# Two of four TensorE transposes moved to a later place in each iteration of a state-space mixer

## The chip, the cores and the metric

The kernel runs on one core of a Trainium2 chip. The metric is the device time of one execution in microseconds, taken as the median of several runs. Three runs of the kernel before gave 1757.22, 1758.23 and 1759.07 us.

## What is computed

The reference is one block of a recurrent model: a layer norm, a mixer of the Mamba-2 kind (`_L0_attn_ref`), a gated feed-forward branch with ternary weights, and their product added to the input. Cut to what bears on the change:

```python
xn = _layernorm(x, axis=-1)                       # x: 4 batches x 256 positions x 512
zxbcdt = xn @ in_proj_w.T                         # gate, xBC, dt
conv = conv1d(xBC, conv_w, 4 taps, causal)
x, B, C = split(silu(conv + conv_b))              # x: 128 heads of 64
xs = x * dt[..., None]
Gm = einsum(C, B)                                 # scores of a chunk
Y_diag = einsum(Gm * L, xs)                       # L: decay from position to position
Y_off = ...                                       # what earlier chunks hand on
y = (Y_diag + Y_off + D * x) * silu(gate)
y = y * rsqrt(mean(y * y over a group) + EPS) * norm_w
s = y @ out_proj_w.T
g = silu(ffn(xn))
return x + s * g
```

All of it is float32. The products `L @ xs` need `xs` with positions on the partitions, while the convolution leaves `x` with channels on the partitions. So `x` is transposed on TensorE, and this is what the change is about.

## The kernel before

**Stages.** The kernel first does the layer norm, the feed-forward branch, the steps dt and the scores of all groups (`front`, to about 310 us). Then comes the main loop (line 766): 64 iterations, one for each tile of 128 of the 8192 inner channels, i = 0 to 63. A tail with no loop over tiles finishes the output projection. The order of all work is written out by hand (`tc.manual_schedule()`): each engine carries out its instructions in the order in which the lines issue them, and waits on semaphores where data or a buffer is not ready.

**One iteration** overlaps three tiles. For tile i it projects gate and x, for tile i-1 (`old`) it computes the recurrence, for tile i-2 (`older`) it gates and squares. From i = 10 on it also does a piece of the output projection of an earlier group (`og >= 0`): the seven block products of one batch in a pair of iterations, four in the even one and three in the odd one. In even iterations VectorE first makes four sums for it (`left_sums`, lines 701 to 704). In every eighth iteration (i = 10, 18, ... 58) TensorE also sums squares in 16 small matmuls (`norm_sums`, L683).

**The projection** of a tile is a fast product of 2 x 2 blocks (Winograd's form of Strassen's method) with seven block products in place of eight. A block product is two calls and appears in the profile as four matmul instructions of 128x512 (`product`, L173). They go into three PSUM banks px, pq and pz. The seven, by their usual numbers, and in the order of issue on TensorE, are:

- P1 = a11 x11 into px; ScalarE copies px to pz (L820)
- P5 = s1 t1 into pq
- P6 = s2 t2, added into px; ScalarE copies px out to gT (L830)
- first half of P2 = a12 x21, added into pz (k = 0, line 836)
- **four transposes of "block 0"** of tile i-1: the first 128 positions of each of the four batches, into the bank tp (`transposed`, L624)
- P7 = s3 t3, added into px: it may write only when L830 has read px (line 845)
- second half of P2 (k = 1, line 846); ScalarE copies px out to xpad (L847)
- P4 = a22 t4, added into px: it may write only when L847 has read px (line 877)
- P3 = s4 x22, added into pq: it may write only when VectorE has read pq (L870, `xpad <- xpad + pq`)
- four transposes of "block 1" of tile i-1 (`values_1`), into the same PSUM bank as block 0

**Who uses the transposes of block 0.** `values_0` (L632) on VectorE scales tp twice; it is issued behind L870. The bank (pool `ps_t`) has one buffer, so block 1's transposes wait for L632.

**Iterations 1 to 9** (`lead`, i - 1 < LEAD) differ: the last activation of tile i-1 and both exponentials of the decay stand on ScalarE between the copies L820 and L830 or right behind, with loads of ScalarE's function tables.

**VectorE** in an iteration, in order: gating (L672), a decay scan (L612), `meet` (L618, L619, twice each), in even iterations the four sums, L870, L632 twice, L886, the scaling of block 1 (L641), the convolution taps (L181), the sums for the next tile's factors, and another scan.

Before the change, the place in the loop reads:

```python
                product(pz, a12, x21, False, (0,))
            if old:
                tp0 = transposed(xTs[i - 1], 0)
```

Of the kernel before, what the change touches and what calls it, by code (L numbers as in the profile page):

```python
# [43 lines left out]
F32 = mybir.dt.float32  # L44
# [6 lines left out]
P = 128  # L51
NB = 4
# [29 lines left out]
def mixer_ffn(ctx: ExitStack, tc: tile.TileContext, x, in_w, conv_w, conv_b, dt_bias, a_log, d_col,  # L82
# [7 lines left out]
    ps_t = ctx.enter_context(tc.tile_pool(name="ps_t", bufs=1, space=PSUM))  # L90
# [76 lines left out]
    def by_batch(v):  # L167
        return v.rearrange("p (b l) -> p b l", l=L)

    def product(pp, a, b, start, ks=range(KT // 2)):  # L170

        for k in ks:
            nc.tensor.matmul(pp, a[:, k, :], b[:, k, :], start=start and k == 0,  # L173
                             stop=k == KT // 2 - 1, skip_group_check=not start)
# [442 lines left out]
    def meet(m, off):  # L617
        nc.vector.tensor_mul(m, m, gm[:, 0:T])  # L618
        nc.vector.tensor_mul(off, off, gm[:, T:])  # L619

    def transposed(xT, c):
        tp = ps_t.tile([P, NB, P], F32, name="tp", tag="t")
        for b in range(NB):
            nc.tensor.transpose(tp[:, b, :], xT[:, b, c * P:(c + 1) * P], ident)  # L624
        return tp

# [11 lines left out]
    def values_1(ct, xT):  # L638
        tp = transposed(xT, 1)
        v = xsp.tile([P, NB, 2, HD], F32, name="v")  # L640
        nc.vector.tensor_tensor(  # L641
            v, tp.rearrange("p b (h d) -> p b h d", d=HD),
            dt[:, 1, :, 2 * ct:2 * ct + 2].unsqueeze(3).to_broadcast([P, NB, 2, HD]), ALU.mult)
        return v

    def y_begin(ct, xT):

        ps = []
        for i in range(2):
            py = ps_y.tile([P, 2, L], F32, name="py", tag="y")  # L650
            nc.scalar.mul(py, xT[:, 2 * i:2 * i + 2, :], dcol[:, ct:ct + 1])
            ps.append(py)
        return ps
# [107 lines left out]
    with tc.manual_schedule():  # L761
        nc.sync.dma_start(gm, scores[0])
        ms, offs = {0: load_rows(0)}, {0: load_off(0)}
        xTs, gTs, yps, wos, rights, toms = {}, {}, {}, {}, {}, {}
        sqacc = rs = ya = outs = left = nxt = ob = sa = sb = sc = None
        for i in range(CT):
            r, g = i % PER_G, i // PER_G
            here, old, older = True, i >= 1, i >= 2
# [66 lines left out]

                product(pz, a12, x21, False, (0,))
            if old:
                tp0 = transposed(xTs[i - 1], 0)
                meet(ms[i - 1][0], offs[i - 1][0])
                meet(ms[i - 1][1], offs[i - 1][1])  # L840
                if r == 0 and here:
                    nc.sync.dma_start(gm, scores[g])
                yps[i - 1] = y_begin(i - 1, xTs[i - 1])
            if here:
                product(px, s3, t3, False)
                product(pz, a12, x21, False, (1,))
                nc.scalar.copy(xpad_h[1], by_batch(px))  # L847
            if og >= 0 and on == 0:
                sd = norm_sums(sqacc)
# [101 lines left out]
        decay_exp(ms[last][1])  # L951
        py = y_begin(last, xTs[last])
        vs = values_0(last, transposed(xTs[last], 0))
        for m, off in zip(ms[last], offs[last]):
            meet(m, off)
# [123 lines left out]
```

## Time and profile before

| | |
|---|---|
| median of three runs | 1758.23 us (1757.22 to 1759.07) |
| the profiled execution | 1757.47 us, span 1755.8 us |
| TensorE clock granted over the span | 0.999 |
| TensorE waiting to load weights of px until ScalarE's copy L847 | 36.8 us in 57 waits |
| four transposes, from the first's start to the next product's | 0.44 us |
| an odd iteration, 909.58 to 930.70 us | 21.1 us |
| an even iteration, 930.70 to 953.56 us | 22.9 us |

The page of the profile gives busy time by engine, the chain of work that ended last, and groups of instructions. PE is TensorE's matmuls, PEld its weight loads (which run ahead of the matmuls), DVE is VectorE, ACT ScalarE. A timeline line has the start in microseconds from the start of the span, the length, engine, line of the kernel, operation, output and inputs, shapes and count; in brackets stands how long the engine was idle before and what released it. [...] An idle of 0.24 us before a weight load of a 128x512 matmul is the normal interval of the stream.

### The profile page before, as it was taken

Reading aid. Unit: us, or ns where it says so; the run is one execution under the profiler, and the core shown is the slowest. Engines: PE = TensorE matmul, PEld = TensorE weight load, DVE = VectorE, ACT = ScalarE, POOL = GpSimd, SP = SyncE. Lnnn points to the kernel's source line nnn. Section 1 sums busy time; section 2 is a strip of 40 time slices with the busy share of each in tenths; the row PEclk is TensorE's granted clock in tenths of the full one; section 3 lists DMA queues with packets and bytes.
Section 4 is the critical chain, followed back from the end, with each engine's and each line's share of the span. In section 5 each row is a group of like instructions: output and inputs, shape, how many; then the busy total and the mean of one; then the engine's idle time right before and its main releaser. Section 6 shows DMA issues by size and latency. Waiting matters only on the chain.

```text
span 1755.8 us, 22590 instructions
## 1 busy us (share of the span) xinstructions
PE 1725.9 (98%) x8494; PEld 1105.4 (63%) x8494; DVE 1449.8 (83%) x1742; ACT 1065.8 (61%) x1418; POOL 197.3 (11%) x238
## 2 busy tenths in 40 slices
PE   9999999999999999999999999999999999999999
PEld 6566667444456666666666666666666666666677
DVE  5757665699988898889888988888888988888876
ACT  4544333577766666666666666666666666666640
POOL 3221121000000000111011101110111011101110
PEclk9999999999999999999999999999999999999999
DMA  6254553567756666776677667766777677767785
GB/s 228 79 189 154 208 180 113 191 209 233 217 197 207 201 206 190 209 201 185 204 210 201 193 183 213 200 199 183 211 201 214 165 213 201 213 165 212 213 233 170
DMA packets 164091, 342.16 MB, mean 195 GB/s; under 512 B 15376, under 2 KB 55952, under 8 KB 163984
## 3 DMA queue, kind: packets, MB, share of 16 engines
q1 hardware_dynamic: 141296, 287.78, 47.4%
q0 software_dynamic: 22688, 52.96, 17.0%
q8 instruction: 67, 1.10, 0.3%
q14 instruction: 40, 0.33, 0.1%
HBM read 236.08 MB, written 76.28 MB: 178 GB/s over the span
## 4 chain that ended last, share of the span: by engine, by line
PE 86%; DVE 10%; ACT 2%; issue 2%; DMA 0%; SPq 0%; ACTq 0%; DVEq 0%
PE px L173 25%; PE po L721 22%; PE pq L173 13%; PE py L665 9%; PE pz L173 6%; PE pp L285 4%; PE tp L624 3%; DVE m L612 2%; PE pf L293 2%; DVE xT L181 2%; PE pg L460 1%; DVE cT L181 1%; PE pv L683 1%; DVE m L618 1%; DVE bT L181 1%
## 5 line engine op out<-in xcount | busy, mean ns | idle before, releaser
L612 DVE TENSOR_TENSOR_SCAN m<-m,after 128x1024 f32<-128x1024 f32 x128 | 292.1, 2282 | 0.0
L173 PE MATMUL px<-xc,w 128*128 128x512 f32 x576 | 279.3, 607 | 4.6 <-ACT xpad L424 2.4
L181 DVE SCALAR_TENSOR_TENSOR xT<-xpad,cw,xT 128x1024 f32<-128x1024 f32 x192 | 246.2, 1282 | 4.6
L721 PE MATMUL po<-wo,ya 128*128 128x256 f32 x768 | 176.5, 379 | 0.0
L173 PEld LDWEIGHTS px<-xc,w 128*128 128x128 f32 x576 | 99.2, 190 | 115.1 <-issue 69.4
L665 PE MATMUL py<-m,v 128*64 128x128 f32 x2048 | 160.6, 276 | 3.7 <-DVE v L641 3.7
L618 DVE TENSOR_TENSOR m<-m,gm 128x1024 f32<-128x1024 f32 x128 | 154.8, 1209 | 1.4 <-ACT m L615 1.4
L721 PEld LDWEIGHTS po<-wo,ya 128*128 128x128 f32 x768 | 141.5, 190 | 17.1 <-issue 0.2
L905 POOL DMA_DIRECT2D sqacc<-sq x54 | 46.1, 853 | 897.5 <-ACT sq L861 894.0
L173 PE MATMUL pz<-xnT,w 128*128 128x512 f32 x288 | 145.8, 592 | 0.0
L173 PE MATMUL px<-xnT,w 128*128 128x512 f32 x288 | 142.0, 615 | 0.4 <-DMA w<-in_in_w 0.4
L173 PE MATMUL px<-xc,s 128*128 128x512 f32 x288 | 135.8, 594 | 4.5 <-ACT cpad L424 2.0
L173 PE MATMUL pq<-xnT,s 128*128 128x512 f32 x288 | 136.2, 595 | 3.4 <-DVE xpad L870 3.4
L615 ACT ACTIVATE m<-m 128x1024 f32<-128x1024 f32 x128 | 135.4, 1058 | 0.7
L173 PE MATMUL pq<-xc,s 128*128 128x512 f32 x288 | 135.4, 592 | 0.2 <-DMA s<-early 0.2
L665 PEld LDWEIGHTS py<-m,v 128*64 128x64 f32 x2048 | 116.9, 137 | 25.6 <-issue 19.7
L721 PE MATMUL po<-tw,sy 128*128 128x256 f32 x512 | 115.9, 379 | 0.0
L624 PEld LDWEIGHTS tp<-ident,xT 128*128 128x128 f32 x512 | 63.8, 141 | 67.4 <-issue 53.2
L721 PEld LDWEIGHTS po<-tw,sy 128*128 128x128 f32 x512 | 97.2, 190 | 13.2
L870 DVE TENSOR_TENSOR xpad<-xpad,pq 128x512 f32<-128x512 f32 x64 | 43.7, 683 | 68.5 <-ACT xpad L847 68.5
L830 ACT COPY gT<-px 128x512 f32<-128x512 f32 x64 | 37.3, 583 | 103.5 <-PE px L173 103.5
L173 PEld LDWEIGHTS px<-xc,s 128*128 128x128 f32 x288 | 54.2, 190 | 72.1 <-issue 65.5
(181 smaller groups left out, 3105.2 us busy)
## 6 DMA issues: line engine op xcount, KB each, us to landing
m<-rows SPq DMA_DIRECT2D x128, 512.0 KB, 6.5
w<-in_in_w SPq DMA_DIRECT2D x133, 256.0 KB, 6.9
mo<-rows SPq DMA_DIRECT2D x128, 256.0 KB, 7.2
gated<-yg SPq DMA_DIRECT2D x64, 512.0 KB, 8.3
ya<-gated SPq DMA_DIRECT2D x30, 1024.0 KB, 7.1
sqacc<-sq POOLq DMA_DIRECT2D x54, 512.0 KB, 5.6
wo<-in_out_w SPq DMA_DIRECT2D x64, 256.0 KB, 7.2
acc<-sa POOLq DMA_DIRECT2D x23, 512.0 KB, 5.9
```

Source lines behind the costliest of these rows:

```text
L173: nc.tensor.matmul(pp, a[:, k, :], b[:, k, :], start=start and k == 0, stop=k == KT // 2 - 1, skip_group_check=not start)
L181: nc.vector.scalar_tensor_tensor(xT, xpad[:, :, k:k + L], cw[:, i, k:k + 1], xT, ALU.mult, ALU.add)
L285: nc.tensor.matmul(pp, w[:, k * P:(k + 1) * P], part[:, k, :], start=(k == 0 and part is xh), stop=(k == KT - 1 and part is xl))
L612: nc.vector.tensor_tensor_scan(m, m, after, 0.0, ALU.add, ALU.mult)
L615: nc.scalar.activation(m, m, AF.Exp)
L618: nc.vector.tensor_mul(m, m, gm[:, 0:T])
L624: nc.tensor.transpose(tp[:, b, :], xT[:, b, c * P:(c + 1) * P], ident)
L665: nc.tensor.matmul(py[d, q * P:(q + 1) * P], v[:, b, h, :], m, start=False, stop=stop, skip_group_check=True)
L721: nc.tensor.matmul(po, a[:, k, :], b[:, k, :], start=start and k == 0, stop=k == HG - 1, skip_group_check=not start)
L830: nc.scalar.copy(gT[:, HALF:], px)
L870: nc.vector.tensor_add(xpad_h[1], xpad_h[1], by_batch(pq))
L905: nc.gpsimd.dma_start(sqacc, sq, accum_op=ALU.add)
```

## The change

`transposed` gets two arguments: which batches to transpose, and a bank to put them in. The main loop calls it twice: for batches 0 and 1 in the old place, and for batches 2 and 3 behind the second half of P2. The call in the tail (line 953) and the one for block 1 (L639) keep all four together.

```diff
-    def transposed(xT, c):
-        tp = ps_t.tile([P, NB, P], F32, name="tp", tag="t")
-        for b in range(NB):
+    def transposed(xT, c, bs=range(NB), tp=None):
+        if tp is None:
+            tp = ps_t.tile([P, NB, P], F32, name="tp", tag="t")
+        for b in bs:
             nc.tensor.transpose(tp[:, b, :], xT[:, b, c * P:(c + 1) * P], ident)
         return tp
@@
             if old:
-                tp0 = transposed(xTs[i - 1], 0)
+                tp0 = transposed(xTs[i - 1], 0, (0, 1))
                 meet(ms[i - 1][0], offs[i - 1][0])
@@
                 product(px, s3, t3, False)
                 product(pz, a12, x21, False, (1,))
+                if old:
+                    transposed(xTs[i - 1], 0, (2, 3), tp0)
                 nc.scalar.copy(xpad_h[1], by_batch(px))
```

## The prediction

> **What bounds the kernel.** I read the page first, to see which engine carries the end; then the waits, to see what that engine waits for; then the timeline of two neighbouring iterations of the main loop.
>
> ```profile
> PE 1725.9 (98%) x8494; PEld 1105.4 (63%) x8494; DVE 1449.8 (83%) x1742; ACT 1065.8 (61%) x1418; POOL 197.3 (11%) x238
> ...
> PE 86%; DVE 10%; ACT 2%; issue 2%; DMA 0%; SPq 0%; ACTq 0%; DVEq 0%
> ```
>
> TensorE is the bound: busy for 98% of the span, and 86% of the chain that ended last. So only what shortens TensorE's own sequence counts. The busy figure hides stalls, however, since a matmul that starts late is drawn as a longer one; I therefore look at starts. The table of waits for weight loads names two of interest:
>
> ```profile
> PEld px L173 <- ACT xpad L847: 36.8, 57, 0.7
> PEld pq L173 <- DVE xpad L870: 20.6, 29, 2.3
> ```
>
> The first is P4's weight load, kept until ScalarE has copied P7 out of the shared bank px. The 0.65 us of such a wait is not all lost, because 0.24 us lies before every weight load of this stream. How much is lost stands in the timeline of TensorE in the iteration from 909.58 to 930.70 us (start, length, engine, line, operands, count):
>
> ```profile
> 914.83 1.02 PE L173 MATMUL pz<-xnT,w 128*128 128x512 f32 x2
> 915.69 0.60 PE L624 MATMUL tp<-ident,xT 128*128 128x128 f32 x4
> 916.13 1.88 PE L173 MATMUL px<-xc,w 128*128 128x512 f32 x4
> 917.85 1.02 PE L173 MATMUL pz<-xnT,w 128*128 128x512 f32 x2
> 918.70 1.97 PE L173 MATMUL px<-xc,w 128*128 128x512 f32 x4
> 920.51 1.88 PE L173 MATMUL pq<-xnT,s 128*128 128x512 f32 x4
> ```
>
> Read from start to start. P7 (916.13) holds its place for 1.72 us, so four matmuls at 0.43. Half of P2 takes 0.86. The four transposes take 916.13 - 915.69 = 0.44, or 0.11 each, though each is drawn 0.27 long: they are pipelined. P4 (918.70) holds its place for 1.81 us, 0.09 more than P7: **that 0.085 us (unrounded) is the stall** in front of P4. In front of P7 there is none, only some 3 ns in changing from transposes to matmuls.
>
> **The change, part by part.** Nothing is added or removed: the same 512 transposes in all, no DMA, no operand. On TensorE's queue two transposes per iteration move past P7 and past half of P2, to the place before P4. SP's and POOL's queues hold nothing of theirs.
>
> 1. *P7 starts earlier by two transposes*, 2 x 0.109 = 0.22 us, if the bank px is free. It is freed by the copy L830:
>
> ```profile
> 915.03 0.59 ACT L830 COPY gT<-px 128x512 f32<-128x512 f32 x1 [1.89 <-PE px L173]
> ...
> 916.02 0.30 PEld L173 LDWEIGHTS px<-xc,w 128*128 128x128 f32 x2
> ...
> 918.05 0.59 ACT L847 COPY xpad<-px 128x512 f32<-128x512 f32 x1 [1.23 <-PE px L173]
> ...
> 918.68 0.30 PEld L173 LDWEIGHTS px<-xc,w 128*128 128x128 f32 x2 [0.65 <-ACT xpad L847]
> ```
>
> The copy ends at 915.62. Where a load really waits for a copy, at 918.68 after 918.64, it follows it by 0.05. So P7's load could start at 915.67; it starts at 916.02 and would now be at 915.80. A margin of 0.13 us is left, so P7 gains the 0.22 in full. Were the cover gone (a copy later by over 0.13), each further 0.1 us would cost 0.1 per iteration, and from 0.21 on all gain would be lost.
>
> 2. *The place before P4 grows by 0.22 us.* The copy L847 follows P7 and comes 0.22 sooner as well. Counted from P7's start, P4 follows at 1.72 + 0.86 + 0.22 = 2.80; now it is 2.66, stall included (1.72 + 0.86 + 0.085). The load of P4 needs the copy, which is ready 2.55 after P7's start (918.68 - 916.13), and is wanted at 2.80 - 0.11 = 2.69, as a load runs one transpose ahead. So 0.13 us of margin here too, and the stall goes. P4 moves by -0.22 + 2.80 - 2.66 = **-0.08 us**: the stall less 3 ns for one more change from transposes to matmuls.
>
> 3. *What is late next.* Behind P4 stands P3, which waits until VectorE has read pq (L870). In the iteration above, L870 begins at 918.66 with the copy and ends some 0.7 us before P3's load, so P3 takes the whole 0.08. In the next one (930.70 to 953.56) VectorE first makes four sums for the output product, and there:
>
> ```profile
> 940.75 0.68 DVE L870 TENSOR_TENSOR xpad<-xpad,pq 128x512 f32<-128x512 f32 x1
> ...
> 941.48 0.34 PEld L173 LDWEIGHTS pq<-xnT,s 128*128 128x128 f32 x2 [0.51 <-DVE xpad L870]
> 941.63 1.88 PE L173 MATMUL pq<-xnT,s 128*128 128x512 f32 x4
> ```
>
> The load already waits for VectorE, and the matmul follows it by 0.153 us, where a waiting load elsewhere (P4's) needs 0.106. Only the difference is left to gain; over the 20 iterations of this kind the gap is 0.153 to 0.164 us, mean 0.158, so **0.05 us each**. VectorE itself cannot come sooner there: from L886 of the iteration before, which waits for TensorE, it works without a pause.
>
> 4. *The readers of the transposes.* The scaling L632 reads them after L870, at 919.27. The moved pair would start at 918.49 and 918.60 (917.85 - 0.22 + 0.86) and end at 918.87; L632 comes 0.22 sooner, at 919.05. So 0.18 us to spare; without it VectorE would be late, and P3 would not care, as it needs only L870. The next transposes into this bank, at 922.22, wait for L632, done by 920.55.
>
> 5. *The iterations where it differs.* In the seven with the sums of squares (16 small matmuls in front of P4), P4's load waits for nothing: 0 gained, the pair only changes places. In iterations 2 to 9 P7 already waits for its copy, which stands behind two table loads and two activations on ScalarE; P7 stays, P4 comes 0.22 - 0.08 = 0.14 later, and P3, which waits for VectorE by about half a microsecond more than P4 lasts, hides that: 0. In iteration 1 P3 has no such wait, so **0.14 us is lost**.
>
> *The sum:* the main stage is iterations 10 to 63. 27 odd ones x 0.082 = 2.21; 20 even ones x 0.052 = 1.03; 7 x 0; less 0.14: **3.1 us gained**. Against the profiled execution, 1757.47 with a span of 1755.8, that is 1754.4. The median of the runs stands 0.76 above that execution, so 1758.23 - 3.1 = 1755.1, or 0.18% less.
>
> [...] The row gives 0.109 us from transpose to transpose. [...]
>
> ```profile
> 332.12 3.68 PE L173 MATMUL px<-xc,w 128*128 128x512 f32 x4 [2.19 <-ACT gT L830]
> ```
>
> The granted clock is 0.50 from 332.3 to 335.6, after an idle stretch of only 2.19 us, so these matmuls take 0.85 apiece and about 1.7 us are lost. The change makes that stretch 2.41. [...]
>
> **Rivals.**
> - *More than forecast:* the even iterations take the full 0.082 too, because VectorE's order is looser than I read it, or the halved clock of iteration 1 is met less often. 47 x 0.082 = 3.9, so 1754.4 or below. For it: the margins of steps 1 and 2. Against: L870's direct wait.
> - *Nothing gained:* the stall moves from P4 to P3 everywhere, VectorE becoming the bound: 1758.2. For it: 83% busy, and the even iterations already within 0.05 us. Against: 0.7 us of slack in the odd ones.
> - *Slower, by a new wait:* splitting the group gives the second pair a weight load with a wait of its own. The first pair's load has one today, on TensorE's own earlier matmul ("PE px L173", 54 times, at most 0.24 us, the ordinary interval, so free). If the second pair's wait is for the end of P2's half just in front, its load comes 0.59 + 0.05 after that matmul's start and the pair 0.75 after it in place of 0.43: 0.32 lost in 54 iterations, 17 us, less the 3.1: about 1772. It decides as soon as the wait is for that half; one for P7 or older is met in time and free. Against: the four transposes today carry one wait among them, and the pair waits for nothing new.
>
> **How the numbers follow.** Forecast 0.58, more 0.20, nothing 0.10, slower 0.12 (with it, a copy L830 late enough to undo step 1). What a measurement of this kernel can tell from no change is about 0.2%, 3.5 us, just above my forecast: faster by more than that takes four fifths of the second case and, by scatter of the runs, nearly a third of the first, 0.34; slower is 0.11; within is the rest, 0.55. The range: the forecast with a scatter of about 1.2 us either way, widened downward to the full gain: 1753.6 to 1757.0. The other two cases are left out.
>
> **What would show it.** In the profile after: two transposes on each side of P7; from P4's start to P3's 1.72 us in odd iterations; the wait of px for L847 gone from the 47, one for L830 not risen; the wait of pq for L870 kept in the even ones; odd iterations 21.05 us long (21.13 now), even ones 22.80 (22.85). Wrong, if P7 is found waiting for L830, or the second pair starts later than 0.86 us after P2's second half.

## The result, and the profile after

The changed kernel took 1755.0 us in the median of 22 runs (1752.99 to 1756.67), and the kernel before 1759.02 in 22 runs made beside them. The ratio of the means is 0.9981, 95% interval 0.9975 to 0.9988: 0.19% less, or 3.3 us; the medians lie 4.0 us apart. Forecast were 1755.1 us and 0.18% less, or 3.1 us. That the median came within 0.1 us of the forecast is luck in part: the level before was 0.8 us higher than the 1758.23 from which the forecast started, the medians differ by 0.9 us more than forecast, and the two cancel.

The page of the changed kernel has TensorE where it was, 2.7 us less busy in a span that is 2.4 us shorter:

```profile
PE 1723.2 (98%) x8494; PEld 1106.2 (63%) x8494; DVE 1449.3 (83%) x1742; ACT 1068.0 (61%) x1418; POOL 196.8 (11%) x238
...
PE 86%; DVE 10%; ACT 2%; issue 2%; DMA 1%; SPq 0%; ACTq 0%; DVEq 0%
```

The table of waits of weight loads shows which wait went. Lines of the kernel have moved by one to three: L850 is the former L847, L831 the former L830, L873 the former L870. First a line of before that the prediction does not show, then three of after:

```profile
PEld px L173 <- ACT gT L830: 3.1, 2, 2.4
```

```profile
PEld pq L173 <- DVE xpad L873: 21.6, 29, 2.6
...
PEld px L173 <- ACT gT L831: 6.1, 10, 2.6
...
PEld px L173 <- ACT xpad L850: 0.6, 1, 0.6
```

P4's wait for the copy of P7 went from 36.8 us in 57 waits to one of 0.6, in iteration 0, which has nothing to transpose; P3's wait for VectorE stayed; P7's wait for the copy of P6, 3.1 us in two waits before, has risen to 6.1 in ten. The timeline of TensorE in the same odd iteration as before, now from 909.32 us, shows the gain:

```profile
912.85 1.88 PE L173 MATMUL px<-xc,s 128*128 128x512 f32 x4
914.57 1.02 PE L173 MATMUL pz<-xnT,w 128*128 128x512 f32 x2
915.43 0.38 PE L625 MATMUL tp<-ident,xT 128*128 128x128 f32 x2
915.65 1.88 PE L173 MATMUL px<-xc,w 128*128 128x512 f32 x4
917.37 1.02 PE L173 MATMUL pz<-xnT,w 128*128 128x512 f32 x2
918.22 0.38 PE L625 MATMUL tp<-ident,xT 128*128 128x128 f32 x2
918.44 1.88 PE L173 MATMUL px<-xc,w 128*128 128x512 f32 x4
920.16 1.88 PE L173 MATMUL pq<-xnT,s 128*128 128x512 f32 x4
```

Starts are to be read again: four matmuls are drawn 1.88 us long, and the next start comes 917.37 - 915.65 = 1.72 after theirs. From P4 (918.44) to P3 (920.16) it is now 1.72 us, the plain length of four matmuls, where it was 1.81 by the lines (1.802 unrounded). The pair of transposes takes 915.65 - 915.43 = 0.22. The even iteration keeps a part of its stall, and these lines of it say why:

```profile
939.49 1.88 PE L173 MATMUL px<-xc,w 128*128 128x512 f32 x4
...
940.40 0.68 DVE L873 TENSOR_TENSOR xpad<-xpad,pq 128x512 f32<-128x512 f32 x1
...
941.14 0.30 PEld L173 LDWEIGHTS pq<-xnT,s 128*128 128x128 f32 x2 [0.60 <-DVE xpad L873]
941.21 1.92 PE L173 MATMUL pq<-xnT,s 128*128 128x512 f32 x4
...
942.96 0.60 PE L625 MATMUL tp<-ident,xT 128*128 128x128 f32 x4
```

P4 ends its place at 939.49 + 1.72 = 941.21. But VectorE is done only at 941.08, P3's load goes at 941.14, and the matmul can follow it by 0.106: 941.24, so 0.03 us too late. The profile draws P3 from 941.21 all the same, and longer; the loss shows in its place, 942.96 - 941.21 = 1.75 us and not 1.72. The length of the iterations, from P1 to P1, in microseconds (number of iterations in brackets):

| | odd, 11 to 61 (26) | even without sums of squares (20) | with sums of squares, 18 to 58 (6) | 2 to 8 (7) |
|---|---|---|---|---|
| before | 21.128 | 22.855 | 24.557 | 17.267 |
| changed | 21.046 | 22.804 | 24.559 | 17.267 |

### The profile page after: what moved, and what is told of

Read it like the earlier page. It is cut to its first block, busy times and chain, and to the rows that moved or that the text cites. A ratio compares the mean times of both kernels' runs of the same rounds, so it can differ in the third digit from the quotient of the medians.

```text
span 1753.4 us, 22592 instructions
## 1 busy us (share of the span) xinstructions
PE 1723.2 (98%) x8494; PEld 1106.2 (63%) x8494; DVE 1449.3 (83%) x1742; ACT 1068.0 (61%) x1418; POOL 196.8 (11%) x238
## 4 chain that ended last, share of the span: by engine, by line
PE 86%; DVE 10%; ACT 2%; issue 2%; DMA 1%; SPq 0%; ACTq 0%; DVEq 0%
PE px L173 24%; PE po L722 22%; PE pq L173 13%; PE py L666 9%; PE pz L173 6%; PE pp L285 4%; PE tp L625 3%; PE pf L293 2%; DVE m L612 2%; DVE xT L181 2%; PE pg L460 1%; DVE cT L181 1%; PE pv L684 1%; DVE m L618 1%; DMA m<-rows 1%
## 5 line engine op out<-in xcount | busy, mean ns | idle before, releaser
L173 PE MATMUL px<-xc,w 128*128 128x512 f32 x576 | 274.4, 599 | 6.2 <-ACT xpad L424 2.9
L625 PEld LDWEIGHTS tp<-ident,xT 128*128 128x128 f32 x512 | 67.7, 141 | 100.9 <-issue 86.6
L831 ACT COPY gT<-px 128x512 f32<-128x512 f32 x64 | 37.4, 584 | 103.4 <-PE px L173 103.4
L666 PE MATMUL py<-mo,v 128*64 128x128 f32 x1024 | 99.5, 273 | 0.0
```

What stands on the lines that cost most here:

```text
L666: nc.tensor.matmul(py[d, q * P:(q + 1) * P], v[:, b, h, :], m, start=False, stop=stop, skip_group_check=True)
L831: nc.scalar.copy(gT[:, HALF:], px)
```

## Experiments

All are edits of the changed kernel; the times in microseconds are medians, the ratios are to runs of the kernel before on the same chip. Iteration lengths come from the profiled execution, where they repeat within 0.002 us in odd iterations. The kernels e5 and e6 ran once each (1756.28 and 1756.94 us) and are read by their profiles alone.

**How much cover is needed.** Three kernels moved one (e1), three (e2) and all four transposes (e3). The edit of e1:

```diff
-                tp0 = transposed(xTs[i - 1], 0, (0, 1))
+                tp0 = transposed(xTs[i - 1], 0, (0, 1, 2))
...
-                    transposed(xTs[i - 1], 0, (2, 3), tp0)
+                    transposed(xTs[i - 1], 0, (3,), tp0)
```

> One transpose stands before P4 and three before P7. My theory (the gain is the wait of P4 for the copy L847, and any cover that outlasts it will do): P4's load is ready 2.55 us after P7's start and is wanted at 1.72 + 0.86 + 0.11 - 0.11 = 2.58, so one transpose is enough: odd iterations 21.05 us, even ones 22.80, the same as with two, and about 3.1 us less than before (ratio 0.9982). Rival (each transpose moved buys its share of the cover): half the gain, odd iterations 21.09, ratio 0.9991.

> Three stand before P4 and one before P7. My theory: P7's load is ready 0.05 us after the copy L830, at 0.84 us after the start of P2's first half, and is wanted at 0.86, so P7 just escapes a wait: odd iterations 21.05, even ones 22.80, ratio 0.9982 again. Rival (P7's cover is used up): P7 waits for L830 by up to 0.1 us, odd iterations 21.1 or more.

> All four stand before P4, none before P7. My theory: the stall only changes its place. P7's load wants to go at 0.43 after the start of P2's first half and may at 0.84, so P7 starts at 0.95 where 0.86 would be possible, 0.09 lost; P4 waits for nothing. Odd iterations 21.13, even ones 22.85 to 22.86, as before the change; iteration 1 loses 0.35; ratio 1.000. Rival (the later the transposes, the better, as P7 and what hangs on it comes sooner): at or below the 21.05 of two moved, ratio 0.998 or less.

| moved | odd | even | with sums of squares | ratio (interval) |
|---|---|---|---|---|
| 0 (before) | 21.128 | 22.855 | 24.557 | 1 |
| 1 | 21.046 | 22.800 | 24.559 | 0.9982 (0.9974 to 0.9989) |
| 2 | 21.046 | 22.804 | 24.559 | 0.9981 (0.9975 to 0.9988) |
| 3 | 21.046 | 22.802 | 24.559 | 0.9984 (0.9977 to 0.9990) |
| 4 | 21.127 | 22.855 | 24.641 | 1.0003 (0.9995 to 1.0011) |

One, two and three are the same; none and four are the same. So it is not a gain per transpose: a wait has a length, a cover of one transpose outlasts what was left of it, and the rest buys nothing. With four moved the stall stands in front of P7, as the timeline of that kernel shows for the same odd iteration:

```profile
916.61 1.02 PE L173 MATMUL pz<-xnT,w 128*128 128x512 f32 x2
...
916.81 0.59 ACT L831 COPY gT<-px 128x512 f32<-128x512 f32 x1 [1.89 <-PE px L173]
...
917.45 0.30 PEld L173 LDWEIGHTS px<-xc,w 128*128 128x128 f32 x2 [0.65 <-ACT gT L831]
917.47 1.97 PE L173 MATMUL px<-xc,w 128*128 128x512 f32 x4
...
919.27 1.02 PE L173 MATMUL pz<-xnT,w 128*128 128x512 f32 x2
```

The copy ends at 917.40, P7's load follows at 917.45, and P7 holds its place for 919.27 - 917.47 = 1.80 us, as P4 did before. With three moved, the load still follows the copy by 0.07 us, 0.02 more than the waiting load above. What the expectation missed is the column with sums of squares: there P4 never waited, so that the new stall of P7 costs 0.08 in each of the seven with no gain against it. Iteration 1 lost the 0.35 that was expected: from P7's load to P3 it took 6.53 us, and 6.18 before.

**Whether the second pair waits for anything (e5).**

```diff
                 product(px, s3, t3, False)
+                if old:
+                    transposed(xTs[i - 1], 0, (2, 3), tp0)
                 product(pz, a12, x21, False, (1,))
-                if old:
-                    transposed(xTs[i - 1], 0, (2, 3), tp0)
```

> The changed kernel with the moved pair directly behind P7, ahead of P2's second half. My theory (only the length of the cover between P7 and P4 counts, not its order, and the second pair has no wait of its own): odd iterations 21.05, even ones 22.80, as with the change. Rival (the pair carries a wait for the matmuls just in front, which P2's half hides in the change): directly behind P7 it would wait for P7's end, 0.3 us lost in each, odd iterations 21.3.

Odd iterations 21.046, even ones 22.803. The pair starts where P7's four matmuls end their place, and P2's half 0.22 later. The rival of a new wait falls; the order within the cover does not matter.

**What caps the even iterations.** VectorE's order there was changed (e4, built a second time as e9):

```diff
-            if og >= 0 and (here and on % 2 == 0 or i == CT - 1):
-                left_sums()
...
             if old:
                 vs = values_0(i - 1, tp0)
+            if og >= 0 and (here and on % 2 == 0 or i == CT - 1):
+                left_sums()
```

> The changed kernel with VectorE's four sums of even iterations behind L870 and the two scalings L632, not ahead of them. My theory (in even iterations P3's wait for L870 keeps 0.03 of the 0.08 us): P3 no longer waits, even iterations 22.77 us and not 22.80, odd ones 21.05, 0.6 us less than the change alone in 20 iterations, ratio to before 0.9979. Rival (VectorE is the bound there as a whole): even iterations stay at 22.80 or grow, because what was put off comes late elsewhere.

> The kernel of e4 again. My theory: even iterations 22.77 us, 0.6 us less than e8 in all. Rival: not told apart from e8, within 0.2 us of it.

Even iterations took 22.772 us in both profiles, 0.083 below the kernel before: the full stall. In an even iteration of e4 L871 (the former L870) starts as soon as the copy L850 has ended, and P3 1.72 behind P4, its load waiting for nothing:

```profile
939.37 0.69 DVE L871 TENSOR_TENSOR xpad<-xpad,pq 128x512 f32<-128x512 f32 x1 [1.41 <-ACT xpad L850]
...
939.63 1.88 PE L173 MATMUL px<-xc,w 128*128 128x512 f32 x4
...
941.35 1.88 PE L173 MATMUL pq<-xnT,s 128*128 128x512 f32 x4
```

So the cap was VectorE's order, not its load. The ratios were 0.9975 (0.9965 to 0.9986) and, beside a repetition of the change (e8) on one chip, 0.9973 (0.9961 to 0.9984) against the change's 0.9981 (0.9974 to 0.9987):

> The changed kernel itself, for a direct comparison with the next two on one chip. My theory: 3.1 to 3.4 us less than before, ratio 0.9981; odd iterations 21.05 us, even ones 22.80. Rival (part of the first difference was chance): ratio 0.999 or more.

The medians of the two differ by 1.2 us, twice the 20 x 0.031 = 0.6 us that the order is worth, and the intervals overlap. It is the profiles that show the gain, not the times: from P1 of iteration 10 to P1 of iteration 63 it is 1177.64 us in e8 and 1177.04 in e9.

**Iterations 1 to 9.** With all four in the old place there (e6; `(0, 1) if i > LEAD else range(NB)`):

> The changed kernel with all four transposes in the old place in iterations 1 to 9. My theory (in iteration 1 the change costs 0.14, in 2 to 9 nothing): from the weight load of P7 to the start of P3 in iteration 1 6.18 us as before the change, where the changed kernel shows 6.32; iterations 2 to 8 17.27 us as in both; the rest as in the changed kernel. Rival (the change gains or loses in 2 to 9 too): iterations 2 to 8 differ from 17.27.

Iterations 2 to 8 are 17.266 to 17.270 us as in all kernels, so the change does nothing there. Iteration 1 gave 6.09 us from P7's load to P3, not 6.18; the changed kernel has 6.32. TensorE's clock was halved for 3.4 us in each of the three, from 332.3 before the change and from 333.9 in this execution, where it fell on P2's second half: that took 1.71 us in place of 0.86 and outlasted the copy of P7. So the 0.085 us of P4's stall was missing, which is just the difference; that this is the reason is argued, and the run by itself neither bears the 0.14 us out nor refutes it. They rest on before and after (6.18 and 6.32), where the halved stretch lay whole on matmuls, and on three and four moved, with such a stretch too: 6.42 and 6.53, about 0.11 more for each transpose.

**The stall of iteration 1.** On top of the kernel of e4, ScalarE copies P6 out before the activation and the exponential (e7, built a second time as e10):

```diff
-            if lead:
+            if lead and i > 1:
                 conv_silu(i - 1, xTs[i - 1])
                 decay_exp(ms[i - 1][0])
-            elif old:
+            elif old and not lead:
...
                 nc.scalar.copy(gT[:, HALF:], px)
+                if lead and i == 1:
+                    conv_silu(0, xTs[0])
+                    decay_exp(ms[0][0])
```

> The kernel of e4 with one more edit: in iteration 1 ScalarE copies P6 out to gT (L830 before the change) ahead of the activation and the first exponential, not behind them. Theory A (the 2.2 to 2.4 us that P7 waits for this copy in iteration 1 are on the path, with the halved clock behind them): P7 starts right behind the transposes, P3 is then bound by VectorE and comes about 1.5 us sooner; about 1752.7, ratio to before 0.9966. Theory B (the exponential put off by 0.6 us, or a halved clock in the new gap in front of P3, takes it back): not more than 0.5 us below e4, ratio 0.9972 to 0.9978.

> The kernel of e7 again. Theory A: iteration 1 takes 20.1 us and not 22.0, with no halved clock behind it, and the median is 1.5 us or more below that of e9. Theory B: the time comes back before the iterations from 10 on, median within 0.5 us of e9.

The first time it gave 1752.49 us, ratio 0.9975 (0.9964 to 0.9985), no better than e4 by the ratio; beside the kernel of e4 on one chip 1751.98 against 1753.55, ratio to before 0.9967 (0.9954 to 0.9979). The first comparison fits theory B, the second theory A; with five and six executions whose ranges overlap, the times do not decide. The profiles show what the order does. In TensorE's timeline of e10, then of e8 (the change, in an execution without a halved clock), both in iteration 1:

```profile
329.71 1.88 PE L173 MATMUL px<-xc,w 128*128 128x512 f32 x4
331.43 1.02 PE L173 MATMUL pz<-xnT,w 128*128 128x512 f32 x2
332.29 0.38 PE L625 MATMUL tp<-ident,xT 128*128 128x128 f32 x2
334.46 1.98 PE L173 MATMUL px<-xc,w 128*128 128x512 f32 x4 [1.79 <-ACT xpad L853]
336.28 1.88 PE L173 MATMUL pq<-xnT,s 128*128 128x512 f32 x4
```

```profile
332.47 1.98 PE L173 MATMUL px<-xc,w 128*128 128x512 f32 x4 [2.40 <-ACT gT L831]
334.29 1.02 PE L173 MATMUL pz<-xnT,w 128*128 128x512 f32 x2
335.14 0.38 PE L625 MATMUL tp<-ident,xT 128*128 128x128 f32 x2
335.36 1.88 PE L173 MATMUL px<-xc,w 128*128 128x512 f32 x4
337.08 1.88 PE L173 MATMUL pq<-xnT,s 128*128 128x512 f32 x4
```

P7 comes sooner: from P6's start to P7's it is 3.88 us in e10 and 6.04 in e8. But P4 then waits 1.79 for its own copy, which now stands behind the exponentials. From the second half of iteration 0's P1, where the feed-forward branch ends, to P1 of iteration 2 it takes 31.49 us in e10, 31.44 in e7, and 31.65 in e8 and in e9: about 0.2 us is what the order itself brings, and not the 1.5 of theory A. Iteration 1 alone took 19.60 us in e10, but 19.68 in e9 as well, which had no halved clock either. Where the halved clock comes, as in the first profile of the changed kernel, the same stretch takes 33.35, so 1.70 more. None was found in the loop in the two profiles of this order. From P6 to P4 TensorE's idle stretches are of 0.86 us, before the transposes, and of 1.79, where e8 has 0.46 and 2.40; whether this is the reason is not shown, as e8 had no halved clock in the loop either. A granted clock that rounds to 1.000 was had by 9 of 13 executions of this order, by 5 of 14 of e4's kernel (e4 and e9), which differs in this edit alone, and by 10 of 43 of the change; with so few it is likely, but not settled, that the order makes the halving rarer. How the 1.6 us between the medians of e10 and e9 divide is not shown: the two profiles, both without a halved clock, differ by 1.1 us at iteration 10, and 0.63 of this was there before the loop. It is the fastest kernel of the study, 0.33% below the kernel before.

## Why the prediction was right

1. *P7 earlier by 0.22, with 0.13 of margin:* from P6's start to P7's it was 3.01 us and is 2.80 (from 912.85 to 915.65; before, from the line below to 916.13). The margin is there too: in the profile after, P7's load follows the copy by 0.18 us, where the waiting load of e3 follows it by 0.05. The limit was found where the sum puts it, between three moved (free) and four (stalled).

```profile
913.12 1.88 PE L173 MATMUL px<-xc,s 128*128 128x512 f32 x4
```

2. *P4's stall gone:* P7 to P4 2.79 us, forecast 2.80. An odd iteration gained 0.082, as forecast.
3. *The even iterations capped at 0.05:* measured 0.051 in the mean of 20, and e4 showed the cause by taking it away. The rival "more" falls for the change as it was made, and "nothing gained" with it.
4. *The readers of the transposes:* L633 (the former L632) begins at 918.79 in an iteration that starts 0.26 sooner, so at 919.05 on the old scale, the time forecast in step 4.
5. *The other iterations:* those with sums of squares 24.559 for 24.557; 2 to 8 unchanged; iteration 1 longer by 0.14, with a halved stretch of 3.41 us in both profiles.
6. *The sum:* from P1 of iteration 10 to P1 of iteration 63 the two profiles differ by 1180.81 - 1177.67 = 3.15 us, and the terms give 26 x 0.082 + 20 x 0.051 = 3.15. In the profiled executions as a whole only 2.40 us is seen (1757.47 and 1755.07): iteration 10 began 0.84 us later after the change. 0.28 of this was there when the feed-forward branch ended, 0.14 is the loss of iteration 1, and 0.42 arose in iteration 9. There VectorE's scan waited for a DMA, which it did not before:

```profile
470.83 2.29 DVE L612 TENSOR_TENSOR_SCAN m<-m,after 128x1024 f32<-128x1024 f32 x1 [0.38 <-DMA m<-rows]
```

That wait does not go with the number of transposes moved: it was 0.40 us in e8, the same kernel, 0.47 in e5, and none with one, three or four moved.

Two details were wrong. The list of signs said that the wait for L830 would not rise; it rose from 3.1 to 6.1 us, and step 5 should have told me: in iterations 2 to 9 P7 stays where it is and TensorE reaches it 0.22 us sooner, so it waits longer and nobody minds. And 1758.23 us as the level before came from three runs; 22 put it at 1759.02. The idle stretch of iteration 1, forecast at 2.41 us, was 2.40, but the halved clock that followed the 2.19 before does not come each time: the loop of the changed kernel had a halved stretch in one profile and none in another, and the last section has what the traces show of it.

The row of 0.109 us for a transpose was the price to take, and not the 0.273 us for which one is drawn: groups of one, two, three and four took 0.11, 0.22, 0.33 and 0.44 us. At 0.273 apiece the two moved would already have run into the copy, and not even three did.

## What to carry to other kernels

Work that must be done anyway is the cover for a wait, and it counts only up to the wait's end: put beside each wait just enough to outlast it, reckoned from start to start (here one transpose of 0.11 us did as much as three), and ask of the neighbour that gives the work away whether its own wait then shows. A stall of 0.085 us that no table of busy time shows can be read as the difference of two distances between starts, and what its end brings in 47 iterations was forecast here to within 0.1 us of what the profiles of the loop show. The times of whole executions scatter by over 3 us, and only many of them show a gain of that size. Then look one step further: where the next instruction already waits for another engine, only the slack to that wait is won (0.051 us of the 0.082 in the even iterations).

## What the runs showed of the hardware

Most of the scatter between executions goes with TensorE's clock, halved for stretches of 3.41 us. By the clock granted over the whole execution (rounded), the medians on one chip were: before, 1756.95 us at 1.000 (5 runs), 1757.73 at 0.999 (7), 1759.07 at 0.998 (14); the change beside them (e8), 1753.40 (6), 1754.88 (6), 1756.12 (8). At equal clock the difference is 2.9 to 3.6 us each time. The profiles say what the steps are: four have no halved stretch before TensorE's last matmul (clock 1.000), three have one (0.999), five have two (0.998 or 0.997).

The 13 stretches stand in two places: eight behind the stall of P7 in iteration 1, five behind one in iteration 10, where P6 waits 1.2 to 2.2 us, depending on the execution, for ScalarE's copy L821 (the former L820). A line of iteration 1 in the changed kernel, and one of iteration 10 in e1, both at half clock:

```profile
332.40 3.43 PE L173 MATMUL px<-xc,w 128*128 128x512 f32 x4 [2.40 <-ACT gT L831]
```

```profile
489.21 3.62 PE L173 MATMUL px<-xc,s 128*128 128x512 f32 x4 [2.22 <-ACT pz L821]
```

A stall of 2.40 us in iteration 1 was followed by a halving in one profile of the changed kernel and by none in another. In the first it ends at 332.40, the granted clock is 0.50 from 332.79 to 336.20, and P7 holds its place for 335.62 - 332.40 = 3.22 us. In e8 it ends at 332.47, P7 holds its place for 1.82, and the clock over the whole execution rounds to 1.000. In iteration 10 P6 waited 2.22 us in e1, and a halving followed; it waited 2.10 in the first profile of the changed kernel and 1.73 in that of the kernel before, and none did: there P6 holds its place for 1.82. So in these profiles the length of the stall alone does not tell whether it costs another 1.70 us or not. What decides it no run was made to test.
